# A spectral attention kernel: quarter-length even transforms, a split even inverse, input folds on GpSimd, and a new plan

## The chip, the cores and the metric

The kernel runs on one core of a Trainium2 chip. The metric is device time in microseconds (us). Before the change, three runs took 3823.56 to 3824.99 us, median 3824.26. The engines are named as in the profile: PE (TensorE; PEld is its weight load), DVE (VectorE), ACT (ScalarE), POOL (GpSimd) and SP (SyncE, which issues most transfers).

## The reference, cut

Input x and ctx are 32 batches of 512 tokens of 512 values, float32 throughout.

```python
# attention, per batch; the FFT runs over the 512 tokens
q = layernorm(x) * factor(token)          # a scalar per token
mem = ctx * gain                          # a constant
Q, K, V = q @ Wq.T + bq, mem @ Wk.T + bk, mem @ Wv.T + bv
Qf, Kf, Vf = fft(Q) * filt, fft(K) * filt, fft(V) * filt
QKV = hamilton(hamilton(Qf, Kf), Vf)      # quaternion products, 4 parts of 128 values
x = x + ifft(QKV).real
# feed forward: top-1 of 8 experts, at most 1024 tokens for each
tokens = layernorm(layernorm(x)) * gamma + beta   # eps 1e-5 each
e = argmax(tokens @ gate.T); weight = softmax(...)[e]
out = x + layernorm(x) + weight * (gelu(tokens @ wi[e]) @ wo[e])
```

(The last two lines stand for a residual around a block that keeps its own residual.)

## The kernel before, in words

There are two stages. `attention_and_routing` (L203) handles the 32 batches, which the texts call rows, one after the other. `experts` (L1065) then runs the eight experts. The change touches the first stage.

A transform over tokens is a matrix product with a table. A real input needs only half of its frequencies, and these are split by parity (index c: 0 even, 1 odd). Even frequencies see the sum of the first and the second half of the tokens, odd ones the difference. For each row:

- `load` (L389) brings ctx and x into SBUF, `scale` (L400) normalizes x on ACT, and `fold` (L392) makes the sum and the difference on DVE. Each fold is 128 partitions by 1024 values; the tiles are cs (from ctx) and qs (from x).
- `forward` (L407) transforms on PE. For each of four column blocks it makes the 256 columns of each parity (128 real, 128 imaginary) from two matmuls. ACT copies the PSUM tile to SBUF (cf, qf).
- `project` (L427) multiplies the spectra with a weight: eight matmuls of 512 columns for each of k, q, v and each parity. The PSUM pair comes from `ps_p` with two buffers, so that each projection waits until the one before the last has been read. ACT makes a copy of one half (xz, L458), and DVE adds and subtracts into blk (L465), two operations.
- In the even half, the lane of frequency 256 needs care: `nyquist_lanes` (L471) sends a row through DRAM (SP: nyid, nyi), and POOL adds the bias with an accumulating transfer (L497) and copies three small pieces (L504 to L506).
- `matrix_product` (L512) is the quaternion product on DVE: six operations of 1024 or 1032 values and two of half that, once for q and k and once more with v, for each parity. `components` (L561) makes the spectrum y from it.
- `residual` (L605) runs the inverse on PE: for each of two token blocks, two matmuls for the odd part and two for the even part, all with 128 rows and 512 columns. ACT copies the odd part, DVE adds and subtracts it from the even part in PSUM, and POOL adds x with an accumulating transfer (L625). `residual_last` (L629) does the same for the last row in another order.
- Norm statistics, the normalized token, its transposes, logits, top-1 choice and the rank in an expert follow a row or two later. Four indirect scatters on POOL (L822) write each row's slots.

The order on each engine is written out by hand. `Timeline` collects calls with a planned time, and `in_order` fixes the resulting order on each engine. Planned times do nothing else: an instruction starts when its engine reaches it and its inputs are there. The period of the plan is `ROW = 66.1`, and the start of row b is `base[b]`. The work of three rows is interleaved: a row's second product and its inverse run while the next row is transformed, and its routing runs in the row after that.

Folds of x and ctx for the next row stand at 24.6 and 27.0 us after a row's start, the offset transfer at 39.6, the first product at 46.0.

A float32 matmul appears in the profile as two instructions, and so a transform's 16 calls are 32 instructions.

Of the kernel before, what the change touches and what calls it, by code (L numbers as in the profile page):

```python
# [17 lines left out]
P = 128  # L18
# [11 lines left out]
def _constants():  # L30
# [8 lines left out]

    sig = lambda v: 1.0 / (1.0 + np.exp(-v))  # L40
# [9 lines left out]
    for c in range(2):  # L50
        k = 2 * np.arange(P, dtype=np.int64) + c
        e = np.exp(-2j * np.pi / S * ((np.arange(h)[:, None] * k[None, :]) % S))
        herm = np.zeros(P, np.complex128)
        if c == 0:
            herm[0] = filt3[0].real
            herm[1:] = filt3[k[1:]] + np.conj(filt3[S - k[1:]])
        else:
            herm[:] = filt3[k] + np.conj(filt3[S - k])
        pack = lambda z: np.concatenate([z.real, z.imag], axis=1)
        f, q, i = pack(e), pack(e * herm), pack(e)  # L60
        if c == 0:
            alt = 1.0 - 2.0 * (n % 2)
            f[:, P] = i[:, P] = alt
            q[:, P] = alt * filt3[h].real
        fwd.append(f)
        fwdq.append(q)
        inv.append(i.T * (0.5 * gain * gain / S))

    fwd, fwdq = (np.stack(a, axis=1) for a in (fwd, fwdq))
    inv = np.stack([a.reshape(2, P, h) for a in inv]).transpose(2, 0, 1, 3)  # L70
# [41 lines left out]
class Timeline:  # L112
# [19 lines left out]
    def run(self):  # L132
        while self.heap:
            t, _, f, args = heapq.heappop(self.heap)
            more = f if hasattr(f, "__next__") else f(*args)
            if hasattr(more, "__next__"):
# [66 lines left out]
def attention_and_routing(tc, a, gain, ident, gamma, beta, tokbuf, meta):  # L203
# [11 lines left out]
    ROW = 66.1  # L215
    base = [0.0] + [58.2 + ROW * b for b in range(B + 2)]
    end = base[B]
    marks = {}
    with ExitStack() as es:
# [26 lines left out]
        places = lambda ap: ap.rearrange("(t p) c f -> p c t f", p=P)  # L246
# [5 lines left out]
        fwd = fwdp.tile([P, 2, H, 2 * P], F32, name="fwd")  # L252
        fwdq = fwdp.tile([P, 2, H, 2 * P], F32, name="fwdq")
        inv = wp.tile([P, 2, 2, HS], F32, name="inv")
# [27 lines left out]
        def offsets():  # L282
# [8 lines left out]
            for i, n in enumerate("qkv"):  # L291
                by = S * FILTER0 if n == "q" else S / gain
                src = plain[:, i, :].rearrange("o (j h f) -> o h f j", h=2, j=2)
                for k, (h, sign) in enumerate(((0, 1), (0, 1), (1, 1), (1, -1))):
                    nc.vector.tensor_scalar(
                        t[:, i, k, :].rearrange("o (f j) -> o f j", j=2), src[:, h], sign * by, None, ALU.mult
                    )
                    yield 0.31
# [23 lines left out]
        def load_stats(b):  # L322
            w[b]["xs"] = xsp.tile([P, TC, D], F32, tag="xs", name=f"xs_{b}")
            nc.sync.dma_start(w[b]["xs"], tok_rows(x_in[b]))
# [19 lines left out]

        def factors(b0, b1):

            n = (b1 - b0) * TC
            most = 8 * TC
# [36 lines left out]
            tt(flat(off), flat(fac), nm, ALU.mult)  # L385
# [7 lines left out]
        def fold(b, n, tag, c):  # L393

            if c == 0:
                w[b][tag] = foldp.tile([P, 2, H, D], F32, tag=tag, name=f"{tag}_{b}")
            src = w[b][n]
            tt(w[b][tag][:, c], src[:, 0:H, :], src[:, H:TC, :], (ALU.add, ALU.subtract)[c])
# [9 lines left out]
        def forward(b, src, table, tag, t):  # L408

            def mm(dc):  # L410
# [3 lines left out]
                for c in range(2):  # L414
                    for i in range(H):
                        nc.tensor.matmul(  # L416
                            ps[:, c * HS : (c + 1) * HS],
                            w[b][src][:, c, i, dc * P : (dc + 1) * P], table[:, c, i, :],
                            start=(i == 0), stop=(i == H - 1),
                        )  # L420

            for dc in range(DC):
                at(t + 1.75 * dc, mm, dc)
                at(t + 1.75 * (dc + 1) + 0.05, lambda dc=dc: nc.scalar.copy(w[b][tag][:, dc, :], w[b]["ps", tag, dc]))
# [172 lines left out]
        def inverse(b, t, c, ps):  # L597
            for ri in range(2):
                nc.tensor.matmul(  # L599
                    ps, inv[:, c, ri, t * P : (t + 1) * P], w[b]["y"][:, c, ri, :], start=(ri == 0), stop=(ri == 1)  # L600
                )

        def residual(b, t0):

            def mm(t, c):  # L605
                w[b]["ps", t, c] = ps = ps_f.tile([P, D], F32, tag="psf", name=f"att_{b}_{t}_{c}")
                inverse(b, t, c, ps)

            def odd(t):
                w[b]["odd", t] = xzp.tile([P, D], F32, tag="odd", name=f"odd_{b}_{t}", bufs=1)  # L610
                nc.scalar.copy(w[b]["odd", t], w[b]["ps", t, 1])

            def half(t, h, op):
                if t == 0 and h == 0:
                    w[b]["r"] = resp.tile([P, TC, D], F32, tag="r", name=f"r_{b}")
                tt(w[b]["r"][:, h * H + t, :], w[b]["ps", t, 0], w[b]["odd", t], op)

            for t in range(H):
                s = t0 + 3.45 * t
                at(s, mm, t, 1)  # L620
                at(s + 1.75, mm, t, 0)
                at(s + 1.8, odd, t)
                at(s + 3.5, half, t, 0, ALU.add)
                at(s + 4.1, half, t, 1, ALU.subtract)
            at(t0 + 8.4, lambda: nc.gpsimd.dma_start(w[b]["r"], tok_rows(x_in[b]), accum_op=ALU.add))  # L625

        def residual_last(b, t_even, t_odd, dt):


            def even(t):  # L630
                if t == 0:
                    w[b]["even"] = ps_p.tile([P, 2, D], F32, tag="psp", name=f"even_{b}")
                inverse(b, t, 0, w[b]["even"][:, t, :])

            def copy(t, h):
                if t == 0 and h == 0:
                    w[b]["r"] = resp.tile([P, TC, D], F32, tag="r", name=f"r_{b}")
                nc.scalar.copy(w[b]["r"][:, h * H + t, :], w[b]["even"][:, t, :])

            def odd(t):  # L640
                w[b]["ps", t, 1] = ps = ps_f.tile([P, D], F32, tag="psf", name=f"att_{b}_{t}")
                inverse(b, t, 1, ps)

            def add(t, h, op):
                r = w[b]["r"][:, h * H + t, :]
                tt(r, r, w[b]["ps", t, 1], op)

            for t in range(H):
                at(t_even + 1.75 * t, even, t)
                at(t_even + 1.75 * (t + 1) + 0.1, copy, t, 0)  # L650
                at(t_even + 1.75 * (t + 1) + 0.7, copy, t, 1)
                at(t_odd + dt * t, odd, t)
                s = t_odd + dt * (t + 1) + 0.1
                at(s, add, t, 0, ALU.add)
                at(s + 0.6, add, t, 1, ALU.subtract)
                at(s + 1.2, bn, b, t)
                at(s + 1.9, bn, b, H + t)
            at(t_even + 4.6, lambda: nc.gpsimd.dma_start(w[b]["r"], tok_rows(x_in[b]), accum_op=ALU.add))
# [8 lines left out]
        def norms(b):  # L667
# [14 lines left out]
            nc.vector.scalar_tensor_tensor(  # L682
# [4 lines left out]
            marks["norms"] = nc.vector.tensor_scalar(one, r[:, 0, :], 1.0, None, ALU.add)  # L687
# [153 lines left out]
        for c in range(2):  # L841
            at(-7.9 + 0.1 * c, lambda c=c: nc.scalar.dma_start(fwd[:, c], places(a["fwd"])[:, c]))
        at(-7.7, load_stats, 0)
        at(-7.6, load_weight, "k")
        at(-7.5, load, 0, "x", x_in)
        at(-7.4, load_weight, "v")
        at(-7.3, offsets)
        at(-7.1, lambda: nc.sync.dma_start(wave, a["wave"]))
        for c in range(2):
            at(-7.0 + 0.1 * c, lambda c=c: nc.sync.dma_start(fwdq[:, c], places(a["fwdq"])[:, c]))  # L850
        at(-6.8, load_weight, "q")
        at(-6.6, small_tables)
        at(9.8, load_stats, 1)
        at(9.9, load, 1, "ctx", ctx_in)
        at(27.8, load, 1, "x", x_in)
        at(27.9, lambda: nc.sync.dma_start(inv, a["inv"]))
        at(28.0, lambda: nc.sync.dma_start(gate[:, :, 0:E], rows(a["gate"])))
        for t in range(TC):
            at(40.0 + 0.1 * t, lambda t=t: nc.sync.dma_start(meta[t].rearrange("(p c) w -> p c w", p=P), empty))
        for h in range(2):  # L860
            at(4.6 + 1.2 * h, turn_weight, "k", h, nc.vector.tensor_copy)
            at(11.0 + 1.3 * h, turn_weight, "v", h, nc.scalar.copy)
            at(18.2 + 1.3 * h, turn_weight, "q", h, nc.scalar.copy)


        stats(0, 2.1, 4.8)
        ahead = [(0, 22.0, 25.2), (0, 44.2, 47.0), (0, 57.5, 60.5)]
        ahead += [(1, 11.0, 14.0), (1, 22.5, 25.4), (1, 47.0, 49.9), (1, 56.0, 60.2)]
        for b in range(2, B):
            ahead += [(b, 25.6, 43.5)] + [(b, 53.5, 60.2)] * (b < 6)  # L870
        for b, (row, t0, t1) in zip(range(1, B), ahead):
# [3 lines left out]
        steps(9.9, 0.21, factors(0, 1))  # L875
        steps(28.3, 0.21, factors(1, 2))
        steps(base[1] + 8.0, 0.4, factors(2, 4))
        for b in (4, 8, 16, 24):
            steps(base[b - 2] + 3.0, 1.15, factors(b, 2 * b if b < 16 else b + 8))


        for b in range(B):
# [3 lines left out]
            if b == 0:  # L886
                for c in range(2):
                    at(-2.4 + 1.2 * c, fold, 0, "ctx", "cs", c)
                    at(25.2 + 1.2 * c, fold, 0, "x", "qs", c)
                for t in range(TC):  # L890
                    at(21.7 + 0.7 * t, scale, 0, t)
            if b + 1 < B:
                tx, tc_, tq = {0: (50.0, 33.0, 52.6), 1: (36.0, 46.5, 49.0)}.get(b, (17.8, 24.6, 27.0))
                for t in range(TC):
                    at(o + tx + 0.73 * t, scale, b + 1, t)
                for c in range(2):
                    at(o + tc_ + 1.2 * c, fold, b + 1, "ctx", "cs", c)
                    at(o + tq + 1.2 * c, fold, b + 1, "x", "qs", c)
                if b + 2 < B:
                    at(o + tc_ + 2.7, load, b + 2, "ctx", ctx_in)  # L900
                    at(o + tq + 2.7, load, b + 2, "x", x_in)

            forward(b, "cs", fwd, "cf", o)
            if b == 0:
                times = {"k0": (9.6, 13.05, 18.2), "v0": (16.5, 20.0, 25.1), "k1": (23.4, 26.9, 31.6)}
# [370 lines left out]
```

## Time and profile before

| what | value |
|---|---|
| median of three runs | 3824.26 us |
| the profiled execution's own time | 3823.41 us |
| its span, first to last instruction | 3821.7 us |
| mean granted TensorE clock | 0.991 |
| PE, DVE, ACT, POOL busy in the span | 98%, 68%, 33%, 13% |
| start of the first transform of row 0, 1, 2, 3, 31 | 10.55, 72.56, 141.76, 210.08, 2076.91 us |
| first matmul of the experts | 2223.20 us |
| fold on DVE, 128 x 1024 | 1.22 us |
| product operation on DVE, 128 x 1032 | 1.22 us |
| residual operation on DVE, 128 x 512 | 0.69 us |

A line of the profile that names a group of instructions has the engine, the source line, the operation, output<-input by the program's names, the shapes and the count. A busy time is a union of intervals: DVE and PE overlap the end of one instruction with the start of the next, so that a duration of 1.22 us takes 1.14 of the engine. In brackets stands idle time ahead of a group and what ended it.

### The profile page before, as it was taken

The numbers are of one execution on the slowest core, as the hardware profiler recorded it, in microseconds if no ns is written. First come the engines' busy times: TensorE is split into PE (matmuls) and PEld (weight loads), VectorE is DVE, ScalarE is ACT, GpSimd is POOL, SyncE is SP. The second block draws the span as 40 slices with busy tenths as digits, with TensorE's granted clock in tenths as the row PEclk, the third lists the DMA queues.
The fourth block names the chain that finished last, engine by engine and source line by source line (L and its number), as shares of the span: only waits on it lengthen the run. The fifth ranks groups of instructions, "written<-read, shape, count | busy, mean of one in ns | idle before, by whom it ended". The sixth has DMA issues, their size and how long they took to land. (4 is left out here: it accounts for less than half of the span.)

```text
span 3821.7 us, 38354 instructions
## 1 busy us (share of the span) xinstructions
PE 3726.4 (98%) x14208; PEld 2557.3 (67%) x14208; DVE 2616.9 (68%) x4789; ACT 1271.9 (33%) x2358; POOL 488.8 (13%) x433
## 2 busy tenths in 40 slices
PE   8999999999999999999999779999999999999998
PEld 5455555555555555555555368888888888888887
DVE  7898898989889898988989754444444435353532
ACT  5555444443444444343433322212111111111121
POOL 0011111111021111111111111111111111111100
PEclk9999999999999999999999889999999999999999
DMA  5353423233332422222231512122222212121300
GB/s 174 111 122 111 111 78 109 79 101 99 100 100 78 118 79 81 77 89 78 69 98 45 154 42 66 45 66 62 57 76 56 77 40 82 34 78 28 94 1 1
DMA packets 242984, 302.42 MB, mean 79 GB/s; under 512 B 67142, under 2 KB 134598, under 8 KB 242795
## 3 DMA queue, kind: packets, MB, share of 16 engines
q1 hardware_dynamic: 205830, 240.18, 18.9%
q0 software_dynamic: 36416, 59.25, 8.4%
q8 instruction: 112, 1.84, 0.2%
q14 instruction: 76, 0.62, 0.1%
q10 hardware_dynamic: 550, 0.53, 0.0%
HBM read 223.77 MB, written 84.55 MB: 81 GB/s over the span
## 5 line engine op out<-in xcount | busy, mean ns | idle before, releaser
L1039 PE MATMUL r_o<-wo,h 128*128 128x256 f32 x3584 | 781.2, 379 | 0.0
L1039 PE MATMUL r<-xt,wi 128*128 128x256 f32 x3584 | 778.5, 380 | 0.8 <-DVE u L1054 0.8
L1039 PEld LDWEIGHTS r<-xt,wi 128*128 128x128 f32 x3584 | 682.1, 190 | 93.9 <-DVE u L1054 1.1
L1039 PEld LDWEIGHTS r_o<-wo,h 128*128 128x128 f32 x3584 | 677.5, 190 | 90.3
L442 PE MATMUL pp_v<-wv,cf 128*128 128x512 f32 x1024 | 457.3, 595 | 9.7 <-DVE blk L465 6.7
L442 PE MATMUL pp_q<-wq,qf 128*128 128x512 f32 x1024 | 457.2, 595 | 0.0
L442 PE MATMUL pp_k<-wk,cf 128*128 128x512 f32 x1024 | 452.4, 595 | 0.0
L442 PEld LDWEIGHTS pp_v<-wv,cf 128*128 128x128 f32 x1024 | 190.2, 191 | 228.3 <-issue 221.1
L442 PEld LDWEIGHTS pp_k<-wk,cf 128*128 128x128 f32 x1024 | 192.3, 190 | 216.9 <-issue 215.0
L442 PEld LDWEIGHTS pp_q<-wq,qf 128*128 128x128 f32 x1024 | 187.7, 190 | 201.9 <-issue 201.4
L1215 ACT ACTIVATE h<-h 128x512 f32<-128x512 f32 x256 | 159.7, 629 | 474.0 <-DVE h L1047 473.7
L822 POOL DMA_INDIRECT meta<-row,slot x128 | 204.8, 1600 | 389.6 <-DVE slot L812 316.4
L416 PE MATMUL ps_cf<-fwd,cs 128*128 128x256 f32 x1024 | 229.2, 382 | 11.6 <-DMA xs<-in_x 10.5
L599 PE MATMUL att<-y,inv 128*128 128x512 f32 x504 | 227.3, 603 | 6.2 <-DVE y L576 3.8
L416 PEld LDWEIGHTS ps_cf<-fwd,cs 128*128 128x128 f32 x1024 | 196.3, 192 | 52.3 <-issue 14.8
L416 PE MATMUL ps_qf<-fwdq,qs 128*128 128x256 f32 x1024 | 226.2, 379 | 0.0
L1189 POOL DMA_INDIRECT out<-o,tid x64 | 106.5, 1664 | 916.7 <-ACT o L1186 803.1
L416 PEld LDWEIGHTS ps_qf<-fwdq,qs 128*128 128x128 f32 x1024 | 194.6, 190 | 26.9 <-issue 0.5
L497 POOL DMA_DIRECT2D blk<-bias x34 | 32.0, 940 | 1341.7 <-issue 1230.4
L599 PEld LDWEIGHTS att<-y,inv 128*128 128x128 f32 x504 | 91.3, 191 | 140.3 <-issue 114.6
L1047 DVE TENSOR_TENSOR h<-r,u 128x512 f32<-128x512 f32 x192 | 129.0, 686 | 68.4 <-PE r L1039 68.0
L1054 DVE TENSOR_TENSOR u_o<-r_o,p_o 128x512 f32<-128x512 f32 x16 | 11.1, 692 | 239.6 <-PE r_o L1039 239.6
(179 smaller groups left out, 4470.1 us busy)
## 6 DMA issues: line engine op xcount, KB each, us to landing
ctx<-in_ctx SPq DMA_DIRECT2D x32, 1024.0 KB
xs<-in_x SPq DMA_DIRECT2D x32, 1024.0 KB
x<-in_x SPq DMA_DIRECT2D x32, 1024.0 KB
r<-in_x POOLq DMA_DIRECT2D x32, 1024.0 KB, 12.1
tokbuf<-tok SPq DMA_DIRECT2D x32, 1024.0 KB
out<-r SPq DMA_DIRECT2D x32, 1024.0 KB
wi<-in_wi SPq DMA_DIRECT2D x64, 512.0 KB
wo<-in_wo SPq DMA_DIRECT2D x32, 1024.0 KB
```

Of the source, the lines that this page charges most:

```text
L416: nc.tensor.matmul(ps[:, c * HS : (c + 1) * HS], w[b][src][:, c, i, dc * P : (dc + 1) * P], table[:, c, i, :], start=(i == 0), stop=(i == ...
L442: nc.tensor.matmul(w[b][key][:, ri, :], w[b][f][:, dc, lo : lo + P], wt[n][:, dc, :], start=(dc == 0), stop=(dc == DC - 1),)
L497: nc.gpsimd.dma_start(w[b]["blk", 0][0:1, lo:hi, :, 0 : 2 * P], bias[lo:hi].unsqueeze(0), accum_op=ALU.add)
L599: nc.tensor.matmul(ps, inv[:, c, ri, t * P : (t + 1) * P], w[b]["y"][:, c, ri, :], start=(ri == 0), stop=(ri == 1))
L822: nc.gpsimd.indirect_dma_start(out=meta[t], out_offset=bass.IndirectOffsetOnAxis(ap=w[b]["slot"][:, t : t + 1], axis=0), in_=w[b]["row"][: ...
L1039: nc.tensor.matmul(to[:, m, :], lhs(a, m, i), rhs(b, i), start=(i == 0), stop=(i == k - 1))
L1047: tt(c[i], x, y, ALU.add)
L1054: tt(u2, product(6, P6), p1, ALU.add)
L1189: nc.gpsimd.indirect_dma_start(out=a["out"], out_offset=bass.IndirectOffsetOnAxis(ap=tid[:, e, col : col + 1], axis=0), in_=o, in_offset=None,
L1215: [lambda o=o: nc.scalar.activation(o, o, AF.Gelu) for o in out],
```

## The change

- The even frequencies are split again, by their own parity. Those of index 0, 4, 8, ... see the sum of two quarters of the folded tokens, those of 2, 6, 10, ... the difference. `forward` makes each from one matmul of 128 columns, 64 real and 64 imaginary; the odd half stays as it was.
- `fold` has four steps: the odd difference (1024 values), the even sum in place (1024), and then sum and difference of its quarters (512 each). It runs on POOL, except for row 0 and the x of row 1, which stay on DVE.
- The even inverse is four matmuls of 64 rows: partitions 0 to 63 of y and of the table make one PSUM tile, partitions 64 to 127 another. ACT copies one of them into r, and DVE adds and subtracts (two operations). The odd part comes later, with four DVE operations that add it to r or subtract it, in place for one half. The ACT copies of the odd part go.
- The plan has `ROW = 61.0`, with new places for nearly everything. The offset transfer is at 28.4 after a row's start, and the first product at 30.7; the lanes of frequency 256 go in two groups. x and ctx are loaded for a later row when POOL's folds have read them.
- Row 0's statistics are made on DVE, its and row 1's factors together; the weights of k and v are loaded ahead of x and turned on DVE. Some small operations (bias blocks, off, one) move to POOL. Later factors are worked out in batches of other sizes, in steps spread over the rows. The row before the last has its norms and routing after the last row's end.

```diff
-    ROW = 66.1
-    base = [0.0] + [58.2 + ROW * b for b in range(B + 2)]
+    ROW = 61.0
+    base = [0.0] + [53.1 + ROW * b for b in range(B + 2)]
...
-        def fold(b, n, tag, c):
-            if c == 0:
+        def fold(b, n, tag, i, eng=nc.gpsimd):
+            if i == 0:
                 w[b][tag] = foldp.tile([P, 2, H, D], F32, tag=tag, name=f"{tag}_{b}")
-            src = w[b][n]
-            tt(w[b][tag][:, c], src[:, 0:H, :], src[:, H:TC, :], (ALU.add, ALU.subtract)[c])
+            src, to = w[b][n], w[b][tag]
+            out, l, r, op = (
+                (to[:, 1], src[:, 0:H, :], src[:, H:TC, :], ALU.subtract),
+                (src[:, 0:H, :], src[:, 0:H, :], src[:, H:TC, :], ALU.add),
+                (to[:, 0, 0, :], src[:, 0, :], src[:, 1, :], ALU.add),
+                (to[:, 0, 1, :], src[:, 0, :], src[:, 1, :], ALU.subtract),
+            )[i]
+            eng.tensor_tensor(out, l, r, op)
...
-                for c in range(2):
-                    for i in range(H):
-                        nc.tensor.matmul(
-                            ps[:, c * HS : (c + 1) * HS],
-                            w[b][src][:, c, i, dc * P : (dc + 1) * P], table[:, c, i, :],
-                            start=(i == 0), stop=(i == H - 1),
-                        )
+                even = ps[:, 0:HS].rearrange("p (r q f) -> p q r f", r=2, q=2)
+                for i in range(H):
+                    nc.tensor.matmul(
+                        ps[:, HS:], w[b][src][:, 1, i, dc * P : (dc + 1) * P], table[:, 1 + i, :],
+                        start=(i == 0), stop=(i == H - 1),
+                    )
+                for q in range(2):
+                    nc.tensor.matmul(
+                        even[:, q], w[b][src][:, 0, q, dc * P : (dc + 1) * P],
+                        table[:, 0, q * P : (q + 1) * P].rearrange("p (r f) -> p r f", r=2),
+                        start=True, stop=True,
+                    )
...
+        def inverse_even(b):
+            for q in range(2):
+                w[b]["ps", q] = ps_f.tile([P, D], F32, tag="psf", name=f"even_{b}_{q}")
+            for ri in range(2):
+                for q in range(2):
+                    k = slice(q * P // 2, (q + 1) * P // 2)
+                    nc.tensor.matmul(
+                        w[b]["ps", q], inv[k, ri, 0:P], w[b]["y"][k, 0, ri, :], start=(ri == 0), stop=(ri == 1)
+                    )
+        def second(b):
+            w[b]["r"] = resp.tile([P, TC, D], F32, tag="r", name=f"r_{b}")
+            nc.scalar.copy(w[b]["r"][:, 1, :], w[b]["ps", 1])
+        def even(b, t):
+            r = w[b]["r"]
+            tt(r[:, t, :], w[b]["ps", 0], r[:, 1, :], (ALU.add, ALU.subtract)[t])
...
+        def odd(b, t, h, last=False):
+            r = w[b]["r"]
+            part = r[:, (h if last else 0) * H + t, :]
+            tt(r[:, h * H + t, :], part, w[b]["ps", t], (ALU.add, ALU.subtract)[h])
...
-            marks["norms"] = nc.vector.tensor_scalar(one, r[:, 0, :], 1.0, None, ALU.add)
+            nc.gpsimd.tensor_scalar(one, r[:, 0, :], 1.0, None, ALU.add)
...
+                for i in range(4):
+                    at(o + tc_ + (0.0, 2.8, 5.6, 7.0)[i], fold, b + 1, "ctx", "cs", i)
+                    at(
+                        o + (tq, tq + 2.8, tq2, tq2 + 1.4)[i] - (0.0, 1.7, 0.0, 0.8)[i] * (b == 0),
+                        fold, b + 1, "x", "qs", i, (nc.gpsimd, nc.vector)[b == 0],
+                    )
...
-                nyquist_lanes(b, 0, 3, o + 37.2, o + 39.6)
-                pt = 46.0, 55.9, 64.2, 68.3, 78.6, 87.0
+                nyquist_lanes(b, 0, 2, o + 26.0, o + 28.4)
+                nyquist_lanes(b, 2, 3, o + 33.6, o + 36.1)
+                pt = (30.7, 41.0, 49.6, 55.9, 65.8, 74.2) if last else (30.7, 46.6, 56.0, 59.5, 69.5, 80.5)
```

In the changed plan a row's folds of ctx stand at 11.0 to 18.0 us and those of x at 19.5, 22.3, 31.0 and 32.4.

## The prediction

> **What bounds the kernel now.** I read the page's busy shares first, then a table of stages, then one row of TensorE, then VectorE and GpSimd over the same kind of row. The shares:
>
> ```profile
> PE 3726.4 (98%) x14208; PEld 2557.3 (67%) x14208; DVE 2616.9 (68%) x4789; ACT 1271.9 (33%) x2358; POOL 488.8 (13%) x433
> ```
>
> TensorE is busy nearly always, so what its stream loses shows in the time, unless another engine takes over. The stage table (columns: stretch, its length, then PE, PEld, DVE, ACT and POOL busy, clock, DMA share, GB/s) says where:
>
> ```profile
> 10.55:72.56 62.01, 59.64 (x161) 32.94 (x162) 45.31 (x153) 38.64 (x86) 1.61 (x4) 0.97 0.53 190
> 72.56:141.76 69.20, 62.79 (x177) 33.11 (x176) 61.05 (x120) 37.52 (x97) 4.15 (x9) 1.00 0.41 122
> 210.08:276.75 66.67, 65.81 (x212) 36.08 (x211) 57.85 (x108) 35.24 (x74) 9.19 (x9) 1.00 0.42 110
> 2143.00:2223.20 80.20, 33.04 (x105) 16.95 (x104) 52.47 (x144) 21.66 (x33) 21.22 (x19) 0.69 0.70 194
> 2223.20:3821.70 1598.50, 1579.80 (x7413) 1386.66 (x7412) 711.16 (x1056) 308.89 (x527) 180.72 (x122) 0.99 0.18 52
> ```
>
> The lines are rows 0, 1 and 3, the tail of the attention stage, and the experts, which the change leaves alone. Row 3 starts at 210.08 and row 31 at 2076.91: 28 rows of 66.67 us, with TensorE busy for 65.81 and VectorE for 57.85. So both are near full, and GpSimd is nearly empty. One row on TensorE (start, duration, group, and in brackets idle time):
>
> ```profile
> 2076.91 7.07 PE L416 MATMUL ps_cf<-fwd,cs 128*128 128x256 f32 x32
> 2083.82 7.07 PE L416 MATMUL ps_qf<-fwdq,qs 128*128 128x256 f32 x32
> 2090.73 7.03 PE L442 MATMUL pp_k<-wk,cf 128*128 128x512 f32 x16
> ...
> 2113.18 1.07 PE L733 MATMUL lp<-tokT,gate 128*32 128x512 f32 x8
> 2114.17 5.42 PE L599 MATMUL att<-y,inv 128*128 128x512 f32 x12
> 2120.45 1.98 PE L599 MATMUL att<-y,inv 128*128 128x512 f32 x4 [0.86 <-DVE r L616]
> 2122.28 0.95 PE L746 MATMUL lg<-four,tokT 128*128 128x8 f32 x8
> 2123.09 7.11 PE L442 MATMUL pp_k<-wk,cf 128*128 128x512 f32 x16
> ```
>
> From start to start a transform is 32 instructions in 6.91 us, 0.216 each; a 512-column instruction is 0.43; the inverse's 16 take 6.9. The one stall, 0.86, is the inverse waiting for a PSUM buffer. VectorE in another row:
>
> ```profile
> 1107.12 2.35 DVE L398 TENSOR_TENSOR cs<-ctx 128x1024 f32<-128x1024 f32 x2
> 1109.39 2.36 DVE L398 TENSOR_TENSOR qs<-x 128x1024 f32<-128x1024 f32 x2
> 1111.66 1.28 DVE L465 TENSOR_TENSOR blk<-pp_q,xz_q 128x512 f32<-128x512 f32 x2
> 1116.96 1.29 DVE L465 TENSOR_TENSOR blk<-pp_v,xz_v 128x512 f32<-128x512 f32 x2 [4.02 <-ACT xz_v L458]
> 1119.94 1.29 DVE L616 TENSOR_TENSOR r<-att,odd 128x512 f32<-128x512 f32 x2 [1.69 <-issue]
> ```
>
> and, in the same stretch on GpSimd:
>
> ```profile
> 1118.77 0.93 POOL L497 DMA_DIRECT2D blk<-bias  x1 [40.21 <-issue]
> ```
>
> A pair of folds takes VectorE 2.27 us from start to start; a half-size operation about 0.61. The offset transfer of a blk is issued over 6 us before the product that reads it (1125.12), so its landing is hidden.
>
> [...] the eight 512-column instructions of lp, on four 32-column groups, take 0.99 us, where eight at 0.43 would take 3.4. [...]
>
> **The change, part by part.**
>
> Forward transforms. The odd half keeps 16 instructions of 256 columns: 16 x 0.216 = 3.46. The even half becomes 16 of 128 columns. Is the weight load the floor? The lg group's eight instructions with 8 columns and full weights take 0.81, about 0.11 each, and half of 0.216 is 0.11 as well: 16 x 0.11 = 1.76. Sum 5.22, a saving of 1.69 each, 3.4 a row. (If each load took the 0.19 that its row shows as duration, only 0.4 would be saved; lg excludes that.)
>
> Inverse. The odd part keeps 8 instructions, 3.44. The even part is 8 instructions of 64 rows, two row groups into two PSUM buffers. Side by side: 4 x 0.43 = 1.72, and I add 0.13 [...] which is what lp needs over 2 x 0.43. One after the other: 3.44. I take 1.85: saving 6.9 - 3.44 - 1.85 = 1.6. Row content: 65.81 - 3.4 - 1.6 = 60.8.
>
> The 0.86 stall goes, because evens and odds no longer alternate through two buffers. Next late is v's first projection, which needs k's PSUM pair. In the new order VectorE comes to k's blk after the second product of the row before; its operations from the trace are 8.1 for the odd half's first product (six at 1.14, two at 0.61), 3.3 for four row statistics, 1.9 for norms, 1.2 for v's blk and 8.1 for the second product, 22.6 from a start just before the row's; so it comes there at about 22 and is done at 23.8 (two blks, three parts of y), and TensorE asks at 25.1. That is 1.3 us of room, so I keep 0.8 of idle time: row 61.6.
>
> VectorE. Folds away: 4.54. The residual has six operations instead of four: +1.22. 57.85 - 4.5 + 1.2 = 54.5. New on its path is a wait. The first product now directly follows q's blk, and needs the offset transfer that q's blk releases: GpSimd issues it and it lands 2.5 us after issue (median of its issue row), so about 2.8 us. 54.5 + 2.8 = 57.3 of 61.6, still under TensorE, and nothing but that 4.3 is spare.
>
> GpSimd. [...] The queue is: four scatters, the small scale that waits for norms, the four ctx folds, two x folds, offset transfer, spread, two x folds. [...] The folds are due at the next row's start, over 25 us later. Behind them stand SyncE's loads: the ctx load waits for the ctx folds, and the two small row transfers (nyid, nyi) that the spread needs are behind it. [...]
>
> ScalarE loses one copy of 0.59 net; its queue has room. The statistics of the first two rows, weight turns and load order at the start: the same bytes in another order, x after both weights. Taken as nothing, +-8 us. Tail: other order, the plan's last step moves by under 1 us; nothing, +-10.
>
> Sum against the profiled run of 3823.4 (span 3821.7): rows 3 to 30, 28 x 5.07 = 142. Rows 1 and 2, 5.0 each, their stalls kept = 10. Row 0 has no inverse: 3.4. Row 31: two transforms and row 30's inverse, 5.0; its own inverse lies on an idle TensorE. Together 160, so 3663; the median of the runs is 0.9 above the profiled one: 3664.
>
> **The rivals.**
>
> GpSimd's folds hold VectorE up in part. For: of VectorE's 54.5 about three quarters are two-input operations from SBUF, and ctx folds meet the second product. With X us of blocking a row is the larger of 61.6 and 57.3 + X. Between X = 4.3 and 9.4 it is still faster; at X = 7, 64.3: 28 x 2.4 + 15 = 82 less, about 3740.
>
> The slower side: the same mechanism at its full price, at the products in rows 1 to 31. [...] 68.8 a row, 2.1 above before, 30 x 2.1 = 63: about 3885 (3835 to 3930). It decides from X = 9.4, where 57.3 + X passes 66.67. [...] Against: instructions of 1.2 us leave gaps, [...].
>
> The two 64-row matmuls don't overlap, so the inverse saves nothing: 31 x 1.6 = 50 given back, about 3714. Against it: lp.
>
> **How the numbers follow.** Forecast 0.46, with its own range 3650 to 3695 (row 61.2 to 62.4, start and tail). Part blocking 0.22, full blocking 0.24, no overlap 0.08. [...] I keep the forecast without blocking as the likeliest single case. The range for 8 in 10 runs from 3650 up through both middle cases to the near edge of the slower one, 3840. A change under 0.2%, 7.6 us, is what a measurement here can't tell from none: 0.03, from where the middle and the slower case meet. Slower 0.23, faster 0.74.
>
> **What would show it.** Right: rows at 61 to 62 with TensorE over 98% busy; transforms of 5.2 us; the even inverse at 1.7 to 1.9; [...] VectorE's products still at 1.22. Wrong: products of 2 us or more beside a fold, TensorE stalls before v's first projection laid to blk, rows of 64 or more; an even inverse of 3.4; idle time before the first product well above 2.8.

## The result: slower, and the profile after

| what | before | after |
|---|---|---|
| median | 3824.62 us | 4008.89 us |
| span of the profiled execution | 3821.7 us | 4007.6 us |
| start of row 3, of row 31, of the experts | 210.08, 2076.91, 2223.20 us | 222.15, 2259.58, 2408.26 us |
| mean of rows 3 to 30 | 66.67 us | 72.77 us |

The ratio is 1.048, with an interval of 1.046 to 1.050. The 28 rows from 3 on account for 171 of the 186 us between the spans, row 0 for 7.5, rows 1 and 2 for 5, the tail for 2.4. The experts took 1599.3 us, before 1598.5. The busy shares of the changed kernel:

```profile
PE 3637.9 (91%) x14208; PEld 2483.9 (62%) x14208; DVE 2859.9 (71%) x4643; ACT 1252.8 (31%) x2307; POOL 1134.7 (28%) x847
```

TensorE's work has shrunk as planned, and its share has fallen from 98% to 91%: something else sets the pace. The table of stretches (columns as before; row 3, a plain row, the tail, the experts):

```profile
222.15:297.34 75.19, 63.58 (x213) 33.80 (x212) 68.76 (x121) 34.88 (x73) 31.81 (x24) 0.93 0.35 99
...
2259.58:2408.26 148.68, 92.46 (x314) 47.62 (x312) 104.16 (x234) 42.52 (x67) 31.89 (x34) 0.79 0.45 126
2408.26:4007.60 1599.34, 1580.13 (x7413) 1386.76 (x7412) 711.44 (x1056) 309.09 (x527) 181.80 (x122) 0.99 0.19 52
```

```profile
1969.90:2041.79 71.89, 63.11 (x213) 33.86 (x212) 65.70 (x101) 24.15 (x39) 29.41 (x23) 0.95 0.28 74
```

In the plain row VectorE is busy for 65.70 us instead of some 58, although the folds have left it. TensorE in that row:

```profile
1979.06 1.03 PE L445 MATMUL ps_qf<-fwdq,qs 128*128 128x256 f32 x4
1979.93 0.61 PE L450 MATMUL ps_qf<-fwdq,qs 128*128 128x128 f32 x4
1980.37 7.03 PE L476 MATMUL pp_k<-wk,cf 128*128 128x512 f32 x16
...
2003.92 5.24 PE L476 MATMUL pp_v<-wv,cf 128*128 128x512 f32 x8 [8.78 <-DVE blk L499]
...
2013.40 1.99 PE L639 MATMUL even<-y,inv 64*128 64x512 f32 x8
2015.32 1.06 PE L772 MATMUL lp<-tokT,gate 128*32 128x512 f32 x8
```

A column block of a transform takes 1.31 us from start to start (1979.06 to 1980.37), so a transform 5.24; the even inverse takes 1.92. Both parts of the change on TensorE work. All the row's idle time is one stall: v's first projection waits 8.78 us for VectorE to read k's PSUM pair. What VectorE does ahead of that, and GpSimd beside it:

```profile
1984.36 1.22 DVE L579 TENSOR_TENSOR pb<-o,blk 128x1024 f32<-128x1024 f32 x1
1985.49 3.38 DVE L579 TENSOR_TENSOR pa<-o,blk 128x1024 f32<-128x1024 f32 x1
1988.80 3.36 DVE L579 TENSOR_TENSOR pb<-o,blk 128x1024 f32<-128x1024 f32 x1
1992.19 2.17 DVE L582 TENSOR_TENSOR pa<-pa,pb 128x1024 f32<-128x1024 f32 x1
1994.29 2.29 DVE L584 TENSOR_TENSOR pa<-pa,pb 128x1024 f32<-128x1024 f32 x1
1996.61 2.72 DVE L590 TENSOR_TENSOR o<-pa 128x512 f32<-128x512 f32 x1
1999.25 2.82 DVE L592 TENSOR_TENSOR o<-pa 128x512 f32<-128x512 f32 x1
2001.99 0.68 DVE L499 TENSOR_TENSOR blk<-pp_k,xz_k 128x512 f32<-128x512 f32 x1
```

```profile
1984.42 3.36 POOL L427 TENSOR_TENSOR cs<-ctx 128x1024 f32<-128x1024 f32 x1
1987.86 3.21 POOL L427 TENSOR_TENSOR ctx<-ctx 128x1024 f32<-128x1024 f32 x1
1991.16 4.34 POOL L427 TENSOR_TENSOR cs<-ctx 128x512 f32<-128x512 f32 x2
1995.45 3.32 POOL L427 TENSOR_TENSOR qs<-x 128x1024 f32<-128x1024 f32 x1
1998.86 2.66 POOL L427 TENSOR_TENSOR x<-x 128x1024 f32<-128x1024 f32 x1
2006.03 0.96 POOL L531 DMA_DIRECT2D blk<-bias  x1 [4.51 <-DVE blk L499]
```

An operation of 1.22 us becomes 3.38, one of 0.69 becomes 2.72, and the folds of 1024 beside them take 2.66 to 3.36 where the shortest of the run takes 2.35: in this stretch each operation is held beside one fold, for nearly the time that the fold takes undisturbed (2.16 of 2.35 us), and the fold is longer too. A fold of 1024 costs the operation that it meets 2.0 to 2.2 us more (3.38 for 1.22, 2.72 for 0.69), a fold of 512 about 1.0 (2.17 and 2.29 for 1.22). Operations with one input in PSUM were not held: 118 blk operations in the run with half folds, and 132 residual operations in the run with late folds, stand beside a fold and keep 0.68 to 0.69 us. The folds don't come late: GpSimd is through with the first six at 2001.52 and idles for 4.51 us until q's blk releases the offset transfer. Over the run 213 operations are longer than in the profile before, by 356 us in all. (A duration of a held instruction holds its wait; it isn't put down as idle time.)

### The profile page after: what moved, and what is told of

It reads as the page before. It is cut to its first block, busy times and chain, and to the rows that moved or that the text cites. A ratio compares the mean times of both kernels' runs of the same rounds, so it can differ in the third digit from the quotient of the medians.

```text
span 4007.6 us, 38751 instructions
## 1 busy us (share of the span) xinstructions
PE 3637.9 (91%) x14208; PEld 2483.9 (62%) x14208; DVE 2859.9 (71%) x4643; ACT 1252.8 (31%) x2307; POOL 1134.7 (28%) x847
## 5 line engine op out<-in xcount | busy, mean ns | idle before, releaser
L476 PE MATMUL pp_v<-wv,cf 128*128 128x512 f32 x1024 | 520.2, 661 | 265.2 <-DVE blk L499 264.1
L861 POOL DMA_INDIRECT meta<-row,slot x128 | 169.3, 1323 | 425.0 <-DVE slot L851 340.4
L579 DVE TENSOR_TENSOR pa<-blk 128x1024 f32<-128x1024 f32 (+1 forms) x128 | 199.6, 1559 | 87.7 <-DMA blk<-bias 83.4
L427 POOL TENSOR_TENSOR cs<-ctx 128x512 f32<-128x512 f32 (+1 forms) x93 | 237.1, 2562 | 2.4
L766 ACT ACTIVATE tokT<-pt,beta,gamma 128x512 f32<-128x512 f32 x124 | 95.4, 770 | 418.5 <-PE pt L755 418.4
L1195 POOL DMA_INDIRECT g<-tokbuf,gid x64 | 80.2, 1253 | 508.0 <-PE ept L1213 484.4
L579 DVE TENSOR_TENSOR pa<-o,blk 128x1032 f32<-128x1032 f32 (+1 forms) x124 | 214.3, 1728 | 0.1
L579 DVE TENSOR_TENSOR pb<-o,blk 128x1032 f32<-128x1032 f32 (+1 forms) x124 | 214.0, 1726 | 0.0
L584 DVE TENSOR_TENSOR pa<-pa,pb 128x1024 f32<-128x1024 f32 (+1 forms) x128 | 187.1, 1462 | 0.0
L531 POOL DMA_DIRECT2D blk<-bias x64 | 57.8, 903 | 452.1 <-DVE blk L499 431.0
L582 DVE TENSOR_TENSOR pa<-pa,pb 128x1024 f32<-128x1024 f32 (+1 forms) x128 | 184.4, 1440 | 2.0
```

What stands on the lines that cost most here:

```text
L427: eng.tensor_tensor(out, l, r, op)
L476: nc.tensor.matmul(w[b][key][:, ri, :], w[b][f][:, dc, lo : lo + P], wt[n][:, dc, :], start=(dc == 0), stop=(dc == DC - 1),)
L531: nc.gpsimd.dma_start(w[b]["blk", 0][0:1, lo:hi, :, 0 : 2 * P], bias[lo:hi].unsqueeze(0), accum_op=ALU.add)
L579: tt(out, _bc(left, full), right, ALU.mult)
L582: tt(pa[:, :, 0], pa[:, :, 0], pb[:, :, 1], ALU.subtract)
L584: tt(pa[:, :, 1], pa[:, :, 1], pb[:, :, 0], ALU.add)
```

## The experiments

Two theories stood at the start. Holding: GpSimd's reads of SBUF hold VectorE, and its lengthened sum sets the row. Plan: the new order is at fault (its loads, the offset wait), and the lengthened operations only fill time that would be idle. A third, the ring, came up on the way. The letters in the expectations are each run's own; in the first run A is holding and B the plan. Times given without a ratio are of one execution; TensorE's stall is the idle time ahead of v's first projection.

**The folds on VectorE, the rest of the change kept.**

```diff
-        def fold(b, n, tag, i, eng=nc.gpsimd):
+        def fold(b, n, tag, i, eng=nc.vector):
...
-                        fold, b + 1, "x", "qs", i, (nc.gpsimd, nc.vector)[b == 0],
+                        fold, b + 1, "x", "qs", i, nc.vector,
```

> The changed kernel with all folds on VectorE, at the same places of the plan. Theory A ([...]): the products are back at 1.22 us each, VectorE does 54.5 + 7.0 of folds = 61.5 us a row and waits some 3 to 5, so rows of 65 to 67 and 3770 to 3840 us in all. Theory B (the new plan itself is too tight, whatever runs the folds: the offset transfer, and k's blk ahead of v's projection): rows stay at 71 or more, 3980 to 4030. Theory C (GpSimd is merely slow and its folds come late): rows near 62, under 3700.

3802.5 us, ratio to before 0.994 (0.993 to 0.996); rows average 65.7. So the rest of the change is worth something, but little: with 7 us of folds VectorE has no slack. Its operations have their old durations (1.22 to 1.23 us for a product of 1032). VectorE still waits for the offset transfer, and TensorE, in the second line, for k's blk, but for 2.6 us and not 8.8:

```profile
1108.09 1.23 DVE L579 TENSOR_TENSOR pa<-blk 128x1032 f32<-128x1032 f32 x1 [3.01 <-DMA blk<-bias]
```

```profile
1166.34 3.70 PE L476 MATMUL pp_v<-wv,cf 128*128 128x512 f32 x8 [2.62 <-DVE blk L499]
```

**The folds as memsets on GpSimd** (the sums are left out; cs and qs are zero).

```diff
+            if eng is nc.gpsimd:
+                eng.memset(out, 0.0)
+                return
```

> The changed kernel with each GpSimd fold replaced by a memset of the same output on GpSimd: the sums and differences of ctx and x are left out, and GpSimd writes as much but reads nothing. Theory A: VectorE's operations keep 1.22 us throughout, the rows are TensorE's 60.8 and what idle time the plan leaves, 61.5 to 63, 3650 to 3720 in all. Theory B: rows of 71 as before. A third possibility, that writing on GpSimd holds VectorE up as well: products of 2 us beside the memsets, rows of 64 to 68.

3667.4 us. Same queue, same places, same writes, but nothing read: no product or residual operation of VectorE is longer (0.3 us in the whole run). A row takes 61.32 us, and TensorE is busy for all of it:

```profile
1734.97:1796.29 61.32, 61.32 (x213) 33.19 (x212) 53.84 (x101) 24.16 (x39) 15.56 (x23) 1.00 0.33 87
```

This is a row without holding, which the forecast put at 61.6, and the time is near the forecast's 3664. The memsets are shorter than folds (0.94 us for 1024), so the run alone doesn't separate reading from being busy. The next does so in part.

**The folds as copies of one input** (the sums are left out).

```diff
+            if eng is nc.gpsimd:
+                eng.tensor_copy(out, l)
+                return
```

> The changed kernel with each GpSimd fold replaced by a copy of its first input on GpSimd: the sums and differences are left out, GpSimd reads one input instead of two. Theory A (what counts is how long the holder's instruction runs, not how much it reads): a VectorE operation beside a copy is longer by about the copy's own time; if a copy of 1024 takes 1.0 to 1.4 us, products of 2.2 to 2.6 us, about half of the 11.7 us a row that the folds cost, rows of 65 to 67, 3760 to 3850. If one input left room for VectorE's second one: products at 1.22 and rows at 62 to 63.

3779.1 us. A copy of 1024 takes 1.03 us at its shortest, hardly more than the memset, but it reads: 182 operations of VectorE are longer, by 118 us, 3.9 us a row, and rows 3 to 30 average 65.2. So the read is what counts here: 118 us of holding with it, 0.3 without. The holding was less than the half that was expected; a copy takes less than half of the shortest fold's 2.35.

What the holding costs is seen in two neighbouring rows. They have the same holding and the same stall of TensorE, but take 65.47 and 63.80 us. Their groups behind the stall, then the two rows and a part of the first group (columns as before; the clock is the third number from the right):

```profile
1601.43 5.40 PE L479 MATMUL pp_v<-wv,cf 128*128 128x512 f32 x8 [2.20 <-DVE blk L502]
...
1666.93 3.70 PE L479 MATMUL pp_v<-wv,cf 128*128 128x512 f32 x8 [2.21 <-DVE blk L502]
```

```profile
1573.99:1639.46 65.47, 63.27 (x213) 33.85 (x212) 57.75 (x101) 24.14 (x39) 21.52 (x23) 0.97 0.30 81
1639.46:1703.26 63.80, 61.59 (x214) 33.25 (x213) 57.77 (x101) 24.14 (x39) 21.55 (x23) 1.00 0.31 83
1601.62:1605.03 3.41, 3.41 (x5) 1.35 (x5) 1.62 (x4) 0.00 (x0) 1.49 (x5) 0.50 0.08 1
```

So 3.9 us of holding cost 2.5 us of row (63.8 against 61.3); the rest was absorbed by room that TensorE has ahead of v's first projection. In 9 of the rows 13 to 29 the granted clock is halved for 3.41 us behind the stall, and that costs 1.7 us more.

**Before, with only its four folds moved to GpSimd.**

```diff
-            tt(w[b][tag][:, c], src[:, 0:H, :], src[:, H:TC, :], (ALU.add, ALU.subtract)[c])
+            nc.gpsimd.tensor_tensor(w[b][tag][:, c], src[:, 0:H, :], src[:, H:TC, :], (ALU.add, ALU.subtract)[c])
```

> The kernel before with its four folds of 1024 on GpSimd and nothing else changed. VectorE loses 4.5 us of its own work a row. Theory A: each fold costs a VectorE operation beside it about 2.15 us, 8.6 a row, so VectorE has 57.85 - 4.5 + 8.6 = 62 busy and held of 66.67: rows of 67 to 69, 3830 to 3900, slower than before although VectorE was given less to do. Theory B: no VectorE operation is longer, and rows stay at 66.7 or fall a little, 3800 to 3825.

A miss: 4133.1 us, ratio 1.081 (1.079 to 1.083), rows of 76.7. The new plan isn't the whole story, since the old one suffers too. The holding has the expected size, 8.4 to 8.5 us a row in four operations; what it would do to the row was expected far too small. VectorE's sum doesn't explain it: in the row below VectorE idles for 10.91 us, waiting for v's spectrum. Small operations paid the full price as well:

```profile
1933.49 2.32 DVE L673 TENSOR_SCALAR na<-mv 128x4 f32<-128x4 f32 x1
1935.84 2.27 DVE L675 SCALAR_TENSOR_TENSOR na<-na,mv 128x4 f32<-128x4 f32 x1
...
1953.77 3.37 DVE L550 TENSOR_TENSOR pa<-pa,pb 128x1024 f32<-128x1024 f32 x1
1957.17 2.72 DVE L556 TENSOR_TENSOR o<-pa 128x512 f32<-128x512 f32 x1
...
1975.20 1.29 DVE L465 TENSOR_TENSOR blk<-pp_v,xz_v 128x512 f32<-128x512 f32 x2 [10.91 <-ACT xz_v L458]
```

The first two have 4 values for each partition and take 0.16 us undisturbed. They are the start of the norms, and the token, its transposes and TensorE wait for these. TensorE in that row:

```profile
1948.14 0.33 PE L716 MATMUL pt<-ident,tok 128*128 128x128 f32 x1 [0.86 <-ACT tok L694]
1949.33 0.33 PE L716 MATMUL pt<-ident,tok 128*128 128x128 f32 x1 [0.86 <-ACT tok L694]
1950.03 0.33 PE L716 MATMUL pt<-ident,tok 128*128 128x128 f32 x1 [0.38 <-ACT tok L694]
...
1955.09 0.66 PE L716 MATMUL pt<-ident,tok 128*128 128x128 f32 x4 [1.29 <-ACT tokT L727]
...
1963.14 6.44 PE L442 MATMUL pp_v<-wv,cf 128*128 128x512 f32 x8 [3.52 <-DVE blk L465]
```

The five waits sum to 6.9 us, and the last group takes 6.44 instead of 3.60, another 2.8: together 9.7 of the 10.8 us by which this row is longer than a plain row of the kernel before (77.17 against 66.37). That the tokens are late because of the two held operations is read from the order of the chain, and was not tried by itself. Nor is a wait always one fold long. In row 1 of this run one operation waits through all four:

```profile
133.74 11.01 DVE L545 TENSOR_TENSOR pb<-blk 128x1032 f32<-128x1032 f32 x1
```

**The changed kernel without the offset transfer** (from row 2 on the bias of the even half is missing).

```diff
-            at(t_blk, offset)
+            if b < 2:
+                at(t_blk, offset)
```

> The changed kernel with its folds on GpSimd, but the accumulating transfer of the bias into blk is left out from row 2 on (so the bias of the even half is missing there), and the first product doesn't wait for it. Theory A (a row is VectorE's own work, 54.5, plus holding, 11.7, plus its forced waits, of which the offset is 2.75): rows fall from 71.8 to 68.5 to 69.5 and the time to 3905 to 3945. Rival B (the row is a ring that runs through GpSimd's folds, and VectorE's waits only fill up what is left): rows stay above 71 and the time above 3980.

4010.5 us: no gain, so holding in its simple form, in which VectorE's sum sets the row, falls. The wait before the first product is gone, but 2.67 us of idle time stand four operations further on, where the changed kernel had 1.01:

```profile
1935.39 1.23 DVE L580 TENSOR_TENSOR pa<-blk 128x1032 f32<-128x1032 f32 x1
...
1942.72 0.69 DVE L499 TENSOR_TENSOR blk<-pp_v,xz_v 128x512 f32<-128x512 f32 x1 [2.67 <-ACT xz_v L492]
```

So VectorE, done with k's blk, has to wait for v's spectrum anyway: TensorE's two projections of v start only when k's blk is done, and ScalarE's copy follows. That makes a ring, which each row goes round once: k's blk, v's projections, v's blk, and then VectorE's work to the next k's blk. The theory of the ring follows: of VectorE's work, what lies between v's blk and the next k's blk lengthens a row; what lies between k's blk and v's blk has cover, as far as VectorE would otherwise wait for v's spectrum. The time is in rival B's range, but the waits show no ring through GpSimd's folds.

**All folds on GpSimd, but behind the offset transfer.**

```diff
-                    at(o + tc_ + (0.0, 2.8, 5.6, 7.0)[i], fold, b + 1, "ctx", "cs", i)
+                    at(o + (tc_ + (0.0, 2.8, 5.6, 7.0)[i] if b < 2 else (30.7, 30.8, 38.3, 38.4)[i]), fold, b + 1, "ctx", "cs", i)
...
-                        o + (tq, tq + 2.8, tq2, tq2 + 1.4)[i] - (0.0, 1.7, 0.0, 0.8)[i] * (b == 0),
+                        o + (tq, tq + 2.8, tq2, tq2 + 1.4)[i] - (0.0, 1.7, 0.0, 0.8)[i] * (b == 0) if b < 2 else o + 38.5 + 0.1 * i,
```

(the loads of ctx and x follow at 43 and 48)

> The changed kernel with all its folds on GpSimd, but from row 2 on behind the offset transfer and the lanes of frequency 256 in GpSimd's queue (the first two of ctx beside the first product, the others after v's offset), so that none is held ahead of k's blk; ctx and x are loaded later. Theory A (only holding between v's blk and the next k's blk lengthens a row; between k's blk and v's blk some 3 us are hidden beside v's projection): rows of 66 to 70.5, time 3830 to 3965. Rival B (any holding lengthens the row by the same amount, because VectorE's sum sets it): rows of 71 or more, time above 3975.

3872.6 us, rows of 67.2 on the median instead of 72.1, as theory A has it. The operations lose 272 us to holding, 84 less than after, and k's blk comes nearly in time:

```profile
1946.82 3.70 PE L476 MATMUL pp_v<-wv,cf 128*128 128x512 f32 x8 [1.76 <-DVE blk L499]
```

The run refutes rival B's numbers, but it doesn't prove the cover. Of the 4.9 us that a row gains, 2.5 are less holding, and v's first eight matmuls take 3.70 us instead of 5.1 to 6.8, which alone is 1.4 to 3.1.

**Each fold on GpSimd as two of half the size.**

```diff
-            eng.tensor_tensor(out, l, r, op)
+            for h in (slice(0, D // 2), slice(D // 2, D)):
+                eng.tensor_tensor(out[..., h], l[..., h], r[..., h], op)
```

(from row 2 on)

> The changed kernel with each of GpSimd's folds issued as two instructions of half the size, from row 2 on. Theory A (VectorE is held for as long as GpSimd reads, whatever the size of its instructions): the products beside a fold take about 2.3 instead of 3.4 but twice as many are held, VectorE's extension stays at 300 to 420 us and the time at 3990 to 4060. Rival B (a price for each meeting of two instructions, about 2.1 us each): extension 600 or more, time above 4100. Rival C (between shorter instructions VectorE gets through unharmed): extension below 200, time below 3920.

3878.6 us. The time is that of the third case, and the lengthening, some 254 us, lies between the cases. But VectorE doesn't get through unharmed; it takes turns with smaller pieces:

```profile
1943.55 2.30 DVE L583 TENSOR_TENSOR pa<-o,blk 128x1024 f32<-128x1024 f32 x1
1945.78 2.28 DVE L583 TENSOR_TENSOR pb<-o,blk 128x1024 f32<-128x1024 f32 x1
...
1964.36 1.75 DVE L583 TENSOR_TENSOR pa<-blk 128x1032 f32<-128x1032 f32 x1 [4.88 <-POOL blk L544]
```

A product beside a half fold loses 1.1 us instead of 2.2, so that fewer folds are through when k's blk is reached; the rest fall behind it (5.1 us held ahead of k's blk instead of 10.5). The wait before the first product grows to 4.9, and the way from k's blk to v's grows with it, so that this part is not all covered.

**The ring in numbers.** Worked out from the traces, medians over rows 13 to 29: the way from the end of k's blk to the start of v's (k to v), the way from there to the end of the next k's blk (v to k), what of each was holding and what idle time of VectorE, and how long v's first eight matmuls took.

| kernel | k to v | held, idle | v to k | held, idle | row | v's first eight |
|---|---|---|---|---|---|---|
| memsets | 11.97 | 0, 5.4 | 49.4 | 0, 1.2 | 61.3 | 3.60 |
| copies | 11.56 | 0, 5.0 | 53.9 | 3.9, 1.8 | 65.4 | 3.70 or 5.4 |
| after | 11.66 | 1.4, 3.8 | 60.5 | 10.5, 1.8 | 72.1 | 5.1 to 6.8 |
| no offset transfer | 11.68 | 2.0, 3.2 | 60.5 | 10.5, 1.8 | 72.6 | 5.1 to 6.8 |
| half folds | 14.47 | 3.1, 4.8 | 53.0 | 5.1, 0 | 67.8 | 3.7 to 6.8 |
| folds late | 13.20 | 3.4, 3.3 | 54.0 | 6.0, 0 | 67.2 | 3.70 |

With copies, after, and without the offset transfer, the way from k's blk to v's is 9.9 us plus what v's first eight matmuls take over 3.70, in every one of these rows: TensorE and ScalarE set it. The way back is 49.8 to 50.0 us plus what is held in it, in 15 of the 17. So the ring without holding is 59.8 us, and a row is 59.8, plus the holding ahead of k's blk, plus what the slow clock costs: 59.8 + 3.9 = 63.7 or, with 1.7, 65.4 for the copies, and 59.8 + 10.5 + 1.8 = 72.1 after. With memsets the ring is shorter than TensorE's 61.3 us of work, which then sets the row; the difference of 1.5 us is the room that holding can use. With half folds and late folds VectorE itself makes the way from k's blk to v's longer, and this sum doesn't hold.

**A better kernel: the folds on VectorE, where it waits.** All folds go to VectorE, as in the first experiment, and the four of x stand directly behind q's blk, in the offset wait.

```diff
-                        o + (tq, tq + 2.8, tq2, tq2 + 1.4)[i] - (0.0, 1.7, 0.0, 0.8)[i] * (b == 0),
+                        o + (tq, tq + 2.8, tq2, tq2 + 1.4)[i] - (0.0, 1.7, 0.0, 0.8)[i] * (b == 0) if b < 2 else o + 27.7 + 0.1 * i,
```

> The folds on VectorE, as in the run with all folds there, but from row 2 on the four folds of x (two of 1024 and two of 512, 3.5 us of VectorE) stand directly after q's blk, in the 3.0 us in which VectorE waits for the offset transfer. Theory A (VectorE's sum sets the row: 65.7 with the wait empty): 3.0 us of the folds now cost nothing, rows of 61.5 to 63 and 3680 to 3730 us; the wait before the first product shrinks below 0.5. Rival B (another chain, such as the offset transfer or TensorE's buffers, sets the row at about 65): 3780 to 3810, and the 3 us turn up as a wait elsewhere.

3746.8 us, ratio 0.979 (0.978 to 0.981), rows of 63.2; the time is a little above the range expected. TensorE still stalls 1.5 us for k's blk, and VectorE 1.0 for the odd half. So the two quarter folds of ctx, which stood ahead of k's blk, go directly ahead of the odd half:

```diff
-                    at(o + tc_ + (0.0, 2.8, 5.6, 7.0)[i], fold, b + 1, "ctx", "cs", i)
+                    at(o + (tc_ + (0.0, 2.8, 5.6, 7.0)[i] if b < 2 or i < 2 else 41.8 + 0.1 * i), fold, b + 1, "ctx", "cs", i)
```

(the load of ctx follows at 42.3)

> As the run with the folds of x in the offset's wait, and from row 2 on the two quarter folds of ctx (1.2 us) move from before k's blk to directly ahead of the odd half of the residual, where VectorE waits 1.0 us for TensorE; ctx is loaded later accordingly. Theory A (a row is VectorE's way from v's blk round to the next k's blk, and what stands there without cover): k's blk comes 1.2 us earlier, TensorE's stall of 1.5 us before v's first projection falls to below 0.6, rows from 63.1 to 61.8 to 62.5, time 3705 to 3735. Rival B (the later ctx load or another chain takes over): 3740 or more.

3722.1 us, ratio to before 0.973 (0.972 to 0.974), 287 us under the changed kernel. The stall before v's first projection is down to 0.42 us in a plain row, as the ring has it; rows 3 to 30 average 63.0. Both engines are full in a plain row of 62.00:

```profile
1911.19:1973.19 62.00, 61.59 (x214) 33.22 (x213) 60.65 (x109) 24.15 (x39) 11.36 (x15) 1.00 0.22 52
```

## Why the prediction was wrong

**What held.** A transform was put at 5.22 us and takes 5.24; the even inverse at 1.85, and takes 1.92 where one after the other would be 3.44. So these 64-row float32 matmuls, on partitions 0 to 63 and 64 to 127, overlap; the profile before had no such pair, and the rival without overlap is out. A row without holding was put at 61.6 and takes 61.3 with memsets (61.3 of TensorE's work and no idle time, where 60.8 and 0.8 were expected). VectorE's own work was put at 54.5: after, 72.1 less 11.9 held and 5.6 idle is 54.6. The offset wait was put at 2.8 and is 2.76. How long a fold takes on GpSimd was the author's estimate, which no trace of before showed. The shortest took 2.35 us for 1024 and 1.27 for 512; most of 1024 took 3.2 to 3.4, and those of 512 took 1.6 to 2.3: 120 of the 122 of 1024, and 121 of the 122 of 512, stand beside an operation of VectorE that is over 0.3 us longer than undisturbed.

**The step that failed: GpSimd's folds were taken to cost VectorE nothing.** The forecast kept "without blocking as the likeliest single case", since "instructions of 1.2 us leave gaps". Beside the folds there are no such gaps: VectorE's operations follow each other back to back (1984.36 to 2002.67 above), and they are held for 11.9 us a row. The full-blocking rival had the effect, and its size: its row of 68.8 has an X of 11.5 us over the 57.3, and 10.5 + 1.4 = 11.9 was measured. That 11.5 was the author's estimate. Neither it nor the doubt about it had a line of the trace behind it: in a row of the kernel before, GpSimd computed with three small operations alone:

```profile
1119.38 0.54 POOL L504 COPY blk<-nyi 128x12 f32<-128x12 f32 x1
1119.51 0.53 POOL L505 COPY blk<-nyi 128x6 f32<-128x6 f32 x1
1119.68 0.60 POOL L506 TENSOR_SCALAR blk<-nyi 128x6 f32<-128x6 f32 x1
```

**The term that was mis-sized: the 4.3 us that VectorE was to have spare.** The rivals took a row as the larger of 61.6 and 57.3 + X, so that the first 4.3 us of X cost nothing. The copies show that only 1.5 us are free: 3.9 us of holding cost 2.5 of row even where no matmul was slowed. VectorE's spare time is real (5.4 us of idle time between k's blk and v's in the memset run, the offset wait included), but it comes after k's blk, and holding that comes ahead of it can't use it.

A second term was missing: the matmuls behind the stall ran at a lower clock (0.70 over 2003.92 to 2009.16), and took 1.4 to 3.1 us longer in each row. The full price is thus 59.8 + 10.5 + 1.8 and not 57.3 + 11.5: 72 instead of 68.8 a row. Thirty rows of 4 us more are 120 of the 124 us between that rival's 3885 and the measured 4009. For the same reason part blocking at X = 7 wouldn't have been 64.3. As an estimate, with the same share ahead of k's blk (6.2), a row would be 66.0, or 67.7 with 1.7 for the clock: about as long as before, or longer. The turning point lay at 5 to 7 us held there (66.67 - 59.8, with and without 1.7), not at 9.4.

The prediction had the right place in its hands: it gave k's blk 1.3 us of room, and 1.5 is what the runs show. With 10.5 us held ahead of it, k's blk is 9.0 late; the stall is 8.78. The prices were put into VectorE's sum, and not into that wait.

**Smaller terms.** Row 0 was put at 3.4 us less and took 7.5 more. The transform of x waits 8.9 us there, in three pieces, for VectorE's folds of x; with memsets these waits are 5.9 and the row takes 63.9. So 5.7 us come from the folds of row 1's ctx on GpSimd, of which 3.0 are in these waits, and the rest is the new order at the start. The tail was put at nothing and took 2.4 more.

## What to carry to other kernels

Moving work to an idle engine is only a gain if the full engine loses less by it than it is relieved of. Here the folds cost VectorE 6.8 us a row when it made them itself (60.65 us busy in the last run, 53.84 with memsets), and 11.9 when GpSimd made them. Sum an engine's delay along the ring of waits that closes from one iteration to the next, and not over its whole row: idle time behind the critical wait doesn't pay for a delay ahead of it. The cheapest place for work on a full engine is a wait that it already has.

## What the runs showed of the hardware that was not expected

Tiny operations paid the same: a TENSOR_SCALAR of 128 x 4, which has one input from SBUF and takes 0.16 us undisturbed, took 2.32 beside a fold of 1024, and a SCALAR_TENSOR_TENSOR of that size 2.27.

TensorE paid twice for a long stall. With the folds in the offset wait, v's first eight matmuls follow stalls of 1.5 to 1.7 us in a plain row and take 3.70. After stalls of 8.7 to 8.8 us, in the changed kernel, they take 5.1 to 6.8, and the granted clock was 0.70 over such a group (2003.92 to 2009.16). The granted clock over a plain row was 0.95 in the changed kernel and 1.00 with memsets.

The length of the stall alone didn't decide it. With copies, stalls of 2.1 to 2.2 us were followed by a slow group in 9 of the rows 13 to 29 and by 3.70 us in 6, and two stalls of over 3.3 us by 3.70.
